# Two graph layers on one core: the first attention step in paired logits, statistics tile by tile, shifts on GpSimd

## The chip, the cores and the metric

The kernel runs on one core of a Trainium2 chip. The metric is the device time of one execution in microseconds (us). A core has a matrix engine (TensorE, PE in the profile), a vector engine (VectorE, DVE), an engine for activation functions (ScalarE, ACT), a general one (GpSimd, POOL) and SyncE (SP), which here issues transfers. Each engine takes its instructions in a program order of its own and waits on semaphores for the others. TensorE writes to PSUM[...]; the other tiles lie in SBUF.

## The reference

Eight batches of x (2048 nodes x 256 features) pass two layers that share one adjacency matrix (2048 x 2048).

```python
h = relu(layernorm(x))
# layer 0: 4 heads of 64, softmax over each chunk of 256 keys by itself
q, k, v = h @ Wq.T + bq, h @ Wk.T + bk, h @ Wv.T + bv
scores = clip(q @ k.T / sqrt(64), -10, 10);  scores = where(adj == 0, -10, scores)
ctx = sum over 8 chunks of softmax(scores of the chunk) @ v of the chunk
x = x + layernorm(ctx @ Wo.T + bo + h) * gamma + beta
h = relu(layernorm(x))
# layer 1
g = h @ W;  e = leaky_relu(g @ a1 + (g @ a2).T, 0.01);  e = where(adj == 0, -1e9, e)
x = x + relu(softmax(e) @ g)
```

## The kernel before

All arithmetic is float32. The order of the work on each engine is written out by hand: an engine executes its instructions in the order in which the program's calls emit them.

**A batch.** A batch has three stretches: attention (layer 0), the layer change, and layer 1. The 2048 rows are cut in four blocks of 512 (`nb` = 0 to 3; the program calls the four block objects `zero`, `low`, `mid`, `last`), and a block in four tiles of 128 rows (`TB`). While one batch is worked on, the projections q, k, v of the next one (`ahead`) are prepared in its layer change, and the row statistics for them in layer 1 of the batch before (`far`). In the first batch, `ahead`'s statistics are taken during attention.

**Attention.** There are 32 steps (block, chunk of keys) for a batch. A step has four heads, in `ORDER`; heads in places 0 and 2 of it use one half of TensorE's rows, 1 and 3 the other half, so that two heads can be multiplied at once. For each head and step, `logits` (L400) multiplies into one of two PSUM tiles of scores (`ps_s`), `clip` (L440, VectorE) clips and masks them into `e`, which gives the PSUM tile back, and `exponentials` (L449, ScalarE) follows. `add` (L455, GpSimd) adds two key tiles, `sums` (L428) and `values` (L416) multiply on TensorE, `invert` (L460, L461, ScalarE) makes the reciprocal, `scale` (L470, VectorE) applies it and frees the banks of `values` (`ps_n`), and `gather` (L475) adds the product to the context by a transfer issued from GpSimd.

The steps are software-pipelined in frames. Frame f has two halves, `begin(f)` (half number 2f) and `end(f)` (half 2f+1), and works on steps f, f-1, f-2 and f-3 at once. Frames 0 and 1 of a batch have no older step to work on. In the first batch they come before the loop; in the others they are put between the last pieces of layer 1 of the batch before (`begin(0)` and `end(0)` after its piece 12 of 0 to 15, `begin(1)` after 13, `end(1)` after 14).

**Pieces beside attention.** What else has to be done is listed by half in `todo`. A piece marked `first` is emitted at the start of its half, one marked `pe` before or between the logits, all others later: those of a `begin` half come after clips 1 and 2 of the frame, those of an `end` half before clip 3. The class `Between` carries a block from attention to layer 1, with its halves counted from 16 (nb + 1):

- `output` (L577, TensorE) and `take` (L586, VectorE) make the attention's output in two PSUM banks and copy each out.
- `stats` (L259, L260, VectorE, on one tile of 128 rows at a time), `power` (L264, L265, ScalarE: Ln, then Exp) and `shift` (L269, VectorE, four numbers a row) make scale and shift of a norm.
- `scaled` (L607, ScalarE), `gamma`, `beta`, `bias` and `add` (L613, L617, L593, L621, on `self.adder`, which is GpSimd within attention) finish layer 0.
- `stats1`, `power1`, `shift1` and `norm1` (L283, ScalarE) are the norm for layer 1, `turn1` (L292, transposes) and `keep1` (L644, ScalarE) turn its result, `values` (L651) multiplies by W, and `keep` (L659 on ScalarE, L660 on VectorE) copies the bank out: the 256 features, and then the two products with a1 and a2.

**The layer change.** After the last frame the program emits what remains of the four blocks, mixed with `ahead`'s projections (`turn` L292 with the copies L330 and L332, `qk` L344 with the copies L348, `values` L358 with the copy L363). Four PSUM banks take turns there (`ps_m`: `ps_n` and `ps_t` alternately, two buffers each). A new user of a bank waits for the copy that frees it.

**Layer 1.** There are 16 pieces, four for each block. A piece is `weights` (L759 and L765, VectorE) and `products` (L782, TensorE). `finish` (L792 to L799) divides and adds to x. Of the accumulators, those of blocks 0 and 2 lie in the two `ps_s` tiles, those of blocks 1 and 3 in `ps_n` and `ps_t`.

Of the kernel before, what the change touches and what calls it, by code (L numbers as in the profile page):

```python
# [12 lines left out]
AF = mybir.ActivationFunctionType  # L13
ALU = mybir.AluOpType
# [14 lines left out]
def gnn_two_layers(  # L29
# [127 lines left out]
    def first(piece):  # L157

        piece.kind = "first"
        return piece  # L160
# [101 lines left out]
    def norm_power(mv, rn):  # L262

        nc.scalar.activation(rn[:, 0, :], mv[:, :, 1], AF.Ln, bias=eps)  # L264
        nc.scalar.activation(rn[:, 0, :], rn[:, 0, :], AF.Exp, scale=-0.5)  # L265

    def norm_shift(mv, rn):

        nc.vector.scalar_tensor_tensor(  # L269
            rn[:, 1, :], mv[:, :, 0], -1.0, rn[:, 0, :], op0=ALU.mult, op1=ALU.mult  # L270
        )

# [23 lines left out]
    class Projection:  # L296
        def __init__(self, b):
            self.b = b
            self.q = self.k = self.v = None
            self.x, self.mv, self.rn, self.hns, self.hT, self.pt = ({} for _ in range(6))  # L300

# [11 lines left out]
        def shift(self, nb):  # L313
            norm_shift(self.mv[nb], self.rn[nb])

# [63 lines left out]
    class Attention:  # L379
# [97 lines left out]
        def has(self, n):  # L477
            return 0 <= n < len(self.STEPS)

# [76 lines left out]
    class Between:  # L558
# [42 lines left out]
        def shift(self):  # L601
            norm_shift(self.mv, self.rn)

# [27 lines left out]
        def shift1(self):  # L631
            norm_shift(self.mv1, self.rn1)

# [40 lines left out]
        def beside(self, values):  # L674
# [7 lines left out]
                8: [pe(lambda: self.output(0)), pe(lambda: self.output(1)), lambda: self.beta(0)],  # L682
                9: [first(lambda: self.take(0)), first(lambda: self.take(1)), lambda: self.stats([0, 1])],
                10: [lambda: self.stats([2]), lambda: self.beta(1)],
                11: [lambda: self.stats([3])],
                12: [self.power],
# [11 lines left out]
            if self.nb == NNB - 2:  # L698
                return todo
            for t in range(TB):  # L700
                at(21 + t, lambda t=t: self.stats1([t]))
            at(25, self.power1)
            at(26, self.shift1)
            if self.nb == 1 or values:
                at(27, lambda: self.norm1(0))
                at(28, lambda: self.norm1(1))
            if values:
                for c in range(FC):
                    at(32, pe(lambda c=c: self.turn1(c)))
                    at(33, first(lambda c=c: self.keep1(c)))  # L710
                for t in range(TB):
                    at(36 + t // 2 * 2, pe(lambda t=t: self.values(t)))
                    at(37 + t // 2 * 2, first(lambda t=t: self.keep(t)))
# [183 lines left out]

    projs = {0: proj, 1: Projection(1)}
    att = Attention(proj)
    att.begin(0)  # L900
    att.end(0)
    att.begin(1)
    att.end(1)
    unfinished = None
    for b in range(B):
# [79 lines left out]

        last.adder = nc.vector
        mid.stats1(range(TB))
        low.ends(1)
        mid.power1()
        mid.shift1()  # L990
        if ahead:
# [20 lines left out]
            for t2 in range(2):  # L1012
                last.gamma(t2)
                last.add(t2)
            last.stats1(range(TB))
            mid.ends(1)
            last.power1()
# [7 lines left out]
            zero.norm1(1)  # L1025
            zero.ends(0)
            ahead.norm(3, 0)
            ahead.qk(2, 0)
            zero.ends(1)
            ahead.norm(3, 1)  # L1030
# [56 lines left out]
        for i, (nb, j4) in enumerate(pieces1):  # L1087
# [24 lines left out]
            if ahead and i == len(pieces1) - 4:  # L1112
                att = Attention(ahead)
                att.begin(0)
                att.end(0)
            if ahead and i == len(pieces1) - 3:
                att.begin(1)
            if ahead and i == len(pieces1) - 2:
                att.end(1)
        if ahead:  # L1120
# [33 lines left out]
```

## Time and profile before

| | us |
|---|---|
| median of 3 runs | 3686.9 (3685.46 to 3690.95) |
| the profiled execution | 3688.98 |
| its span in the trace | 3687.1 |

| engine | busy us | share |
|---|---|---|
| TensorE, matmuls | 3633.1 | 99% |
| TensorE, weight loads | 2202.9 | 60% |
| VectorE | 2600.7 | 71% |
| ScalarE | 1946.7 | 53% |
| GpSimd | 1781.4 | 48% |

The profile comes from one execution. In the timeline a line gives the start, the duration, the engine and the line of the kernel, the operation, what is written from what is read, how many instructions were merged (x), and in brackets the idle time before it with the engine and line that ended it. In the table of stretches the columns are the length, then the busy time of PE, PEld, DVE, ACT and POOL with the number of instructions, the granted clock of TensorE, the share of the DMA engines and GB/s. Ends of matmuls are modelled: successive matmuls overlap, so the distance of their starts tells more than their durations. A float32 matmul shows as two records.

### The profile page before, as it was taken

What the parts mean: (1) busy time and instruction counts of PE and PEld (TensorE: products, weight loads), DVE (VectorE), ACT (ScalarE), POOL (GpSimd) and SP (SyncE); (2) the same over time, 40 slices, a digit from 0 to 9 for tenths busy, and PEclk for the clock granted to TensorE, in tenths of its full rate; (3) what the DMA queues carried; (4) which work ended last, traced back from release to release, by engine and by line L of the source; (5) the groups of instructions that cost most, each with busy time, mean ns of one, the idle gap of its engine ahead of it and who ended that gap; (6) DMA issues with size and microseconds to landing.
All of it is one profiled execution on the core that took longest, in us unless ns stands there. A gap on an engine that the chain in (4) does not pass through costs nothing.

```text
span 3687.1 us, 99355 instructions
## 1 busy us (share of the span) xinstructions
PE 3633.1 (99%) x43952; PEld 2202.9 (60%) x43952; DVE 2600.7 (71%) x3959; ACT 1946.7 (53%) x2879; POOL 1781.4 (48%) x1098
## 2 busy tenths in 40 slices
PE   8999999999999999999999999999999999999999
PEld 4444785447754477545775457645586545865468
DVE  4887577865777666786667866678576785767766
ACT  4777416773167732676226762367613667147650
POOL 0678016870177702786027850378403774048731
PEclk9999999999999999999999999999999999999999
DMA  4554113340133401343113431134312332123321
GB/s 139 137 128 110 41 52 82 82 107 27 59 85 81 101 29 63 82 99 82 46 47 82 99 76 46 53 82 94 75 52 58 87 83 64 46 53 88 71 58 35
DMA packets 116641, 274.83 MB, mean 75 GB/s; under 512 B 9968, under 2 KB 75248, under 8 KB 108016
## 3 DMA queue, kind: packets, MB, share of 16 engines
q0 software_dynamic: 32256, 117.45, 17.4%
q1 hardware_dynamic: 83952, 151.01, 12.1%
q8 instruction: 344, 5.64, 0.6%
q14 instruction: 89, 0.73, 0.1%
HBM read 130.03 MB, written 20.97 MB: 41 GB/s over the span
## 4 chain that ended last, share of the span: by engine, by line
PE 90%; DVE 5%; ACT 2%; issue 1%; DMA 1%; POOL 1%; SPq 0%; POOLq 0%; DVEq 0%; ACTq 0%
PE ps_s L400 23%; PE ps_n L416 22%; PE ps_s L782 11%; PE ps_n L782 6%; PE ps_t L428 6%; PE ps_t L782 6%; PE ps_t L577 3%; PE ps_s L344 2%; PE ps_n L344 2%; PE ps_t L344 2%; DVE e L440 2%; PE ps_t L358 1%; PE ps_n L358 1%; PE ps_t L292 1%; PE ps_t L651 1%
## 5 line engine op out<-in xcount | busy, mean ns | idle before, releaser
L455 POOL TENSOR_TENSOR both<-e 128x1024 f32<-128x1024 f32 x512 | 1217.4, 2403 | 740.0 <-PE ps_s L400 248.4
L440 DVE SCALAR_TENSOR_TENSOR e<-ps_s,bound 128x1024 f32<-128x1024 f32 x1024 | 1218.7, 1219 | 399.7 <-PE ps_s L400 397.3
L400 PE MATMUL ps_s<-q,k 64*32 64x512 f32 x16384 | 1398.5, 591 | 4.2 <-DVE e L440 3.0
L449 ACT ACTIVATE e<-e 128x1024 f32<-128x1024 f32 x1024 | 1053.4, 1050 | 575.6 <-DVE e L440 553.3
L416 PE MATMUL ps_n<-e,v 64*32 64x512 f32 x16384 | 1182.5, 590 | 2.2 <-DVE prod L470 2.2
L416 PEld LDWEIGHTS ps_n<-e,v 64*32 64x32 f32 x16384 | 449.0, 107 | 501.6 <-issue 417.9
L400 PEld LDWEIGHTS ps_s<-q,k 64*32 64x32 f32 x16384 | 432.8, 106 | 478.2 <-issue 324.7
L799 POOL TENSOR_TENSOR x<-x,r 128x256 f32<-128x256 f32 x128 | 98.5, 770 | 1107.6 <-DVE rz L792 1039.3
L428 PE MATMUL ps_t<-both,ones 64*32 64x512 f32 x4096 | 533.7, 591 | 1.3 <-SPq L372 1.2
L782 PE MATMUL ps_s<-g,w 128*128 128x257 f32 x2048 | 448.7, 380 | 0.0
L782 PEld LDWEIGHTS ps_s<-g,w 128*128 128x128 f32 x2048 | 388.4, 190 | 55.0
L470 DVE TENSOR_TENSOR prod<-ps_n,rz 128x512 f32<-128x512 f32 x448 | 288.3, 685 | 164.5 <-PE ps_n L416 94.8
L765 DVE SCALAR_TENSOR_TENSOR w<-bound,w 128x1024 f32<-128x1024 int8 x256 | 313.7, 1225 | 8.7
L782 PE MATMUL ps_n<-g,w 128*128 128x257 f32 x1024 | 292.6, 382 | 0.0
L759 DVE TENSOR_SCALAR w<-src,cd 128x512 f32<-128x512 f32 x512 | 265.2, 560 | 36.2 <-ACT src L753 35.8
L782 PE MATMUL ps_t<-g,w 128*128 128x257 f32 x1024 | 290.1, 380 | 0.0
L460 ACT ACTIVATE rz<-ps_t 128x512 f32<-128x512 f32 x256 | 152.6, 596 | 179.6 <-PE ps_t L428 129.3
L475 POOL DMA_DIRECT2D ctxT<-prod x224 | 194.4, 868 | 54.8 <-DVE prod L470 53.3
L782 PEld LDWEIGHTS ps_n<-g,w 128*128 128x128 f32 x1024 | 192.7, 190 | 43.4 <-issue 17.6
L782 PEld LDWEIGHTS ps_t<-g,w 128*128 128x128 f32 x1024 | 194.0, 189 | 28.0
L428 PEld LDWEIGHTS ps_t<-both,ones 64*32 64x32 f32 x4096 | 117.9, 106 | 91.1 <-SPq L372 48.5
L461 ACT ACTIVATE rz<-rz 128x512 f32<-128x512 f32 x256 | 161.4, 631 | 8.1
(125 smaller groups left out, 2842.7 us busy)
## 6 DMA issues: line engine op xcount, KB each, us to landing
ctxT<-prod POOLq DMA_DIRECT2D x224, 512.0 KB, 4.8
bound<-bound_d SPq DMA_DIRECT2D x60, 1024.0 KB, 5.3
xp<-in_x_dram SPq DMA_DIRECT2D x60, 512.0 KB, 4.8
rows<-in_adj_dram SPq DMA_DIRECT2D x32, 512.0 KB, 4.7
x<-in_x_dram SPq DMA_DIRECT2D x32, 512.0 KB, 5.2
out_dram<-x SPq DMA_DIRECT2D x31, 512.0 KB, 2.9
bound_d<-bound SPq DMA_DIRECT2D x4, 1024.0 KB, 6.3
out_dram<-x SPq DMA_DIRECT2D x4, 128.0 KB, 1.7
```

Of the source, the lines that this page charges most:

```text
L344: nc.tensor.matmul(pp, w[:, di, do * P:(do + 1) * P], self.hT[nb][:, di, :], start=di == 0, stop=di == FC - 1,)
L400: nc.tensor.matmul(self.s[n, o][c * Q:(c + 1) * Q, kt, :], self.k[p][rows, at:at + Q], self.q[p][rows, nb * NB:(nb + 1) * NB], start=True, ...
L416: made.append(nc.tensor.matmul(self.num[n, c][h * Q:(h + 1) * Q, :], self.v[rows, j * KT + kt, at:at + Q], self.e[n, p][rows, i * KT + kt, :],
L428: nc.tensor.matmul(self.total[n][h * Q:(h + 1) * Q, :], ones[rows, :], self.both[n, h // 2][rows, h % 2, :], start=half == 1, stop=half == 0,)
L440: nc.vector.scalar_tensor_tensor(self.e[n, p][:, i * KT:(i + 1) * KT, :], self.s.pop((n, o)), -CLIP * SC, bounds[nb][:, j * KT:(j + 1) * K ...
L449: nc.scalar.activation(e, e, AF.Exp, scale=1.0 / SC)
L455: nc.gpsimd.tensor_tensor(self.both[n, p], e[:, 0], e[:, 1], op=ALU.add)
L470: nc.vector.tensor_tensor(dst[:, c, :], self.num.pop((n, c)), self.rz[n], op=ALU.mult)
L475: nc.gpsimd.dma_start(self.ctxT[nb], self.prod.pop(n), accum_op=ALU.add)
L759: nc.vector.tensor_scalar(w[:, i, :], self.src[nb], self.cd[:, 0, j:j + 1], self.cd[:, 1, j:j + 1], op0=ALU.mult, op1=ALU.max,)
L765: nc.vector.scalar_tensor_tensor(two, bounds1[nb][:, j - 1:j + 1, :], 0.0, two, op0=ALU.is_gt, op1=ALU.mult)
L782: nc.tensor.matmul(accs[t][:, 0:F + 1], w[:, i, t * P:(t + 1) * P], g[:, j, :], start=j == 0, stop=j == NT - 1,)
```

## The change

1. `Attention.early` replaces frames 0 and 1 of each batch. Its three parts emit the logits of step 0 two heads at a time (0 with 1, 2 with 3, alternating row halves), the clips and exponentials between, and the logits of head 0 of step 1. The places in layer 1 stay (after pieces 12, 13 and 14).
2. `norm_power` gets a third ScalarE instruction, which copies the scale with its sign turned. `norm_shift` becomes a multiplication of two operands, on an engine that is passed in: GpSimd for the blocks in attention and for the second batch's projections, VectorE otherwise.
3. In `beside`, statistics are spread out: `stats` of tiles 0 and 1 follow each one `take`, tile 2 comes in the same half, tile 3 one half later; `stats1` goes from four successive halves (21 to 24) to 20, 22, 26 and 28, and `power1`, `shift1`, `norm1`, `turn1` and `keep1` follow later.
4. In the layer change, the value products and bank copies of `low` and of `mid` stand tile by tile between the statistics of `mid` and of `last`, and `zero`'s transposes stand behind the q projection of `ahead`'s block 2 instead of before it.

```diff
         nc.scalar.activation(rn[:, 0, :], rn[:, 0, :], AF.Exp, scale=-0.5)
-
-    def norm_shift(mv, rn):
-
-        nc.vector.scalar_tensor_tensor(
-            rn[:, 1, :], mv[:, :, 0], -1.0, rn[:, 0, :], op0=ALU.mult, op1=ALU.mult
-        )
+        nc.scalar.activation(rn[:, 1, :], rn[:, 0, :], AF.Copy, scale=-1.0)
+
+    def norm_shift(engine, mv, rn):
+
+        engine.tensor_tensor(rn[:, 1, :], rn[:, 1, :], mv[:, :, 0], op=ALU.mult)
...
+        def early(self, part):
+
+            if part == 0:
+                for kt in range(KT):
+                    self.logits(0, 0, kt)
+                    self.logits(0, 1, kt)
+            elif part == 1:
+                for o in range(2):
+                    self.clip(0, o)
+                    self.exponentials(0, o)
+                for kt in range(KT):
+                    self.logits(0, 2, kt)
+                    self.logits(0, 3, kt)
+            else:
+                self.clip(0, 2)
+                self.exponentials(0, 2)
+                self.clip(0, 3)
+                for kt in range(KT):
+                    self.logits(1, 0, kt)
+                self.add(0, 0)
...
-                9: [first(lambda: self.take(0)), first(lambda: self.take(1)), lambda: self.stats([0, 1])],
-                10: [lambda: self.stats([2]), lambda: self.beta(1)],
-                11: [lambda: self.stats([3])],
+                9: [
+                    first(lambda: self.take(0)), first(lambda: self.stats([0])),
+                    first(lambda: self.take(1)), first(lambda: self.stats([1])), lambda: self.stats([2]),
+                ],
+                10: [lambda: self.stats([3]), lambda: self.beta(1)],
...
-            for t in range(TB):
-                at(21 + t, lambda t=t: self.stats1([t]))
-            at(25, self.power1)
-            at(26, self.shift1)
+            for t, n in enumerate((20, 22, 26, 28)):
+                at(n, lambda t=t: self.stats1([t]))
+            at(29, self.power1)
+            at(30, self.shift1)
             if self.nb == 1 or values:
-                at(27, lambda: self.norm1(0))
-                at(28, lambda: self.norm1(1))
+                at(31, lambda: self.norm1(0))
+                at(32, lambda: self.norm1(1))
             if values:
                 for c in range(FC):
-                    at(32, pe(lambda c=c: self.turn1(c)))
-                    at(33, first(lambda c=c: self.keep1(c)))
+                    at(34, pe(lambda c=c: self.turn1(c)))
+                    at(35, first(lambda c=c: self.keep1(c)))
...
+    projs[1].adder = nc.gpsimd
     att = Attention(proj)
-    att.begin(0)
-    att.end(0)
-    att.begin(1)
-    att.end(1)
+    for part in range(3):
+        att.early(part)
...
-        last.adder = nc.vector
-        mid.stats1(range(TB))
-        low.ends(1)
+        for block in blocks:
+            block.adder = nc.vector
+        for t in range(TB):
+            mid.stats1([t])
+            low.values(t)
+            low.keep(t)
...
-            last.stats1(range(TB))
-            mid.ends(1)
+            for t in range(TB):
+                last.stats1([t])
+                mid.values(t)
+                mid.keep(t)
...
-            zero.ends(0)
             ahead.norm(3, 0)
             ahead.qk(2, 0)
+            zero.ends(0)
             zero.ends(1)
...
             if ahead and i == len(pieces1) - 4:
                 att = Attention(ahead)
-                att.begin(0)
-                att.end(0)
-            if ahead and i == len(pieces1) - 3:
-                att.begin(1)
-            if ahead and i == len(pieces1) - 2:
-                att.end(1)
+            if ahead and i >= len(pieces1) - 4 and i < len(pieces1) - 1:
+                att.early(i - (len(pieces1) - 4))
```

More of the change, by code (lines that the diff above doesn't have):

```diff
@@ L299, in __init__ @@
             self.q = self.k = self.v = None
+            self.adder = nc.vector
             self.x, self.mv, self.rn, self.hns, self.hT, self.pt = ({} for _ in range(6))
@@ L313, in shift @@
         def shift(self, nb):
-            norm_shift(self.mv[nb], self.rn[nb])
+            norm_shift(self.adder, self.mv[nb], self.rn[nb])
         def norm(self, nb, t2):
@@ L601, in shift @@
         def shift(self):
-            norm_shift(self.mv, self.rn)
+            norm_shift(self.adder, self.mv, self.rn)
         def scaled(self, tiles):
@@ L631, in shift1 @@
         def shift1(self):
-            norm_shift(self.mv1, self.rn1)
+            norm_shift(self.adder, self.mv1, self.rn1)
         def norm1(self, t2):
```

## The prediction

> **What bounds the kernel now.** I read the page's totals first, then the busy time by stretch for one whole batch, then the timeline where TensorE has holes. Page, busy time and chain:
>
> ```profile
> span 3687.1 us, 99355 instructions
> PE 3633.1 (99%) x43952; PEld 2202.9 (60%) x43952; DVE 2600.7 (71%) x3959; ACT 1946.7 (53%) x2879; POOL 1781.4 (48%) x1098
> PE 90%; DVE 5%; ACT 2%; issue 1%; DMA 1%; POOL 1%; SPq 0%; POOLq 0%; DVEq 0%; ACTq 0%
> ```
>
> TensorE is the bound, but its 99% comes from modelled ends. I count starts instead: a 512-column matmul follows the last after 0.43 us, one of 256 columns after 0.216, a transpose after 0.109; of quarter matmuls (64*32, two row halves by four column groups) eight share 0.43. With the counts of the groups: 36864 quarters (L400, L416, L428) 1981 us; 5664 of 256 to 258 columns (L782, L577, L651, L358, L728) 1223; 512 of L344 220; 656 transposes and 256 of L211 86. That is 3510 of the 3687.1, so some 177 us are holes, or unpaired halves. One batch, stretch by stretch (layer change, layer 1, attention):
>
> ```profile
> 1278.80:1342.20 63.40, 60.60 (x256) 42.79 (x253) 26.67 (x71) 34.77 (x78) 3.38 (x3) 1.00 0.10 26
> 1342.20:1460.50 118.30, 118.30 (x602) 99.12 (x600) 89.90 (x174) 15.28 (x30) 15.34 (x16) 1.00 0.15 50
> 1460.50:1730.40 269.90, 269.77 (x4609) 131.38 (x4608) 203.28 (x241) 188.95 (x248) 203.63 (x118) 1.00 0.40 92
> ```
>
> By starts the layer change holds 58.8 us of work in 63.4, layer 1 115.5 in 118.2, attention 260.6 in about 268. What the change is worth is what it takes out of those 4.6, 2.7 and 8 us, batch by batch, and a short startup. Clock 1.00 throughout: no gain there.
>
> **Part 1: paired logits in the first step.** Timeline at the end of layer 1: the first step's logits L400 between the products L782.
>
> ```profile
> 1433.51 1.92 PE L400 MATMUL ps_s<-q,k 64*32 64x512 f32 x16
> ...
> 1442.50 1.95 PE L400 MATMUL ps_s<-q,k 64*32 64x512 f32 x32
> ...
> 1451.51 1.97 PE L400 MATMUL ps_s<-q,k 64*32 64x512 f32 x32
> ```
>
> Five units of 16 run as 16, 32, 32. The middle 32 alternate row halves in program order; the last 32 do not (head 3 whole, then the next step's head 0 whole), yet take the same 1.97 us: their starts lie two by two 0.06 us apart. The Trainium skill (TensorE: Matmul & The Clock Gate, "The mechanism") says matmuls keep strict program order; by it the last 32 would need seven slots of 0.43, 3.0 us, and pairing them would save 1.3 us in each of 7 batches, 9 us. The row decides: already paired. After the change the groups are 32, 32, 16: equal, so 0 us. The clips and exponentials move one piece earlier, but TensorE is full around 1460, so nothing follows. The second PSUM tile of scores that step 0 now needs at 1433.5 is free by 1430.2 (ScalarE's last L795).
> Startup, batch 0, is different: there L400 at 73.73 waits in order behind a clip, so the second clip starts at 74.93 instead of 73.7. The new order clips at once; the fourth clip ends about 1 us earlier, and the mask conversions queued behind it (L203, to which TensorE's transposes wait) follow. Bounds 0 to 1.3; I take **-1.0 us**.
>
> **Part 2: bank copies between statistics, layer change.** Timeline:
>
> ```profile
> 1281.39 1.56 POOL L621 TENSOR_TENSOR x<-x,o 128x512 f32<-128x512 f32 x1
> 1281.79 1.03 PE L651 MATMUL ps_n<-w1s,hT 128*128 128x258 f32 x4
> 1282.98 0.43 DVE L259 BATCH_NORM_STATS2 stats<-x 128x6 f32<-128x256 f32 x1 [1.42 <-POOL x L621]
> 1284.25 0.66 PE L292 MATMUL ps_t<-ident,hn 128*128 128x128 f32 x4 [1.43 <-DVE sd L660]
> ...
> 1303.94 0.13 DVE L660 COPY sd<-ps_t 128x2 f32<-128x2 f32 x1
> 1304.12 0.66 PE L292 MATMUL ps_t<-ident,hn 128*128 128x128 f32 x4 [0.64 <-DVE sd L660]
> ...
> 1305.74 4.03 ACT L283 ACTIVATE hn<-x,rn 128x256 f32<-128x256 f32 x8
> 1309.83 0.33 PE L292 MATMUL ps_t<-ident,hn 128*128 128x128 f32 x1 [0.16 <-ACT hn L283]
> ```
>
> Hole A: TensorE is done at 1282.67 (1281.79 + 4 x 0.22) and waits to 1284.25 for a bank, whose 0.15 us copy stands behind four tiles of statistics, the third of which waits for GpSimd. Interleaved, copies 0 and 1 come at 1281.2 and 1282.0 and both transposes run at once; the next product needs copy 2, still behind that third tile: 1282.98 + 0.43 + 0.18 + 0.15, so 1283.9 instead of 1285.18: **1.29 us**.
> Hole B: done at 1303.33, next start 1304.12. The same cure; VectorE and ScalarE come 1.09 us earlier (1.29 less 0.2 for the new Copy, by L265's 205 ns). The value product of 1305.05 starts at 1302.9: 0.86 more, 2.15 together.
> Hole C: zero's transposes wait for eight L283 (1305.74 to 1309.77) and lose 1.04 us. ScalarE can't follow by the whole 2.15: its third-tile wait stays and it has the Copy. L283 would end at 1308.6, TensorE be there at 1306.4. The change puts a 3.44 us q projection in front, until 1309.8; but now transposes and value products of zero stand back to back, and between them ScalarE has still a norm (1.08), two q copies and two bank copies (0.57 each): the second operand at 1312.0, against TensorE at 1310.7. I get 1.12 lost instead of 1.04. Sum 2.15 - 0.08 = 2.07 a batch, **-14.5 us** over 7 batches; bounds 1.3 to 2.9 each (9 to 20). The eighth has no next batch to fill in: its transposes wait for ScalarE's norms anyway (2.84 us in the trace), and the copies and the Copy in three norm chains lengthen that: **+0.5**.
>
> **Part 3: statistics and shift in attention.** A frame of VectorE is 4 x 1.22 + 2 x 0.69 = 6.3 us against 8.05 of TensorE. Where extras bunch, the clip is late:
>
> ```profile
> 1236.05 1.55 POOL L617 TENSOR_TENSOR x<-x,beta_r 128x512 f32<-128x512 f32 x1
> ...
> 1236.37 1.25 DVE L269 SCALAR_TENSOR_TENSOR rn<-mv,rn 128x4 f32<-128x4 f32 x1
> 1237.55 0.42 DVE L259 BATCH_NORM_STATS2 stats<-o 128x6 f32<-128x256 f32 x1
> ...
> 1238.62 2.32 DVE L440 SCALAR_TENSOR_TENSOR e<-ps_s,bound 128x1024 f32<-128x1024 f32 x2
> ```
>
> The shift of four numbers took 1.25 us beside GpSimd's L617, 0.15 elsewhere. Then two tiles of statistics (0.53 each): the clip is about 0.6 late and the scores at 1241.0 lose 0.46 us. In the frame before, three tiles make it 0.2. Both occur for blocks 1 and 2: 1.32 a batch. After: statistics 0 and 1 lie in the two waits for the output products (1.15 and 1.03 us; the second tile ends at 1225.85, the clip's scores at 1226.38), the shift is gone, one tile follows. 7 x 1.32 = 9.2; batch 0, where VectorE is full with L203 at 250 to 266 and loses about 4 us, 2.5. Bounds 4 and 15; I take 11.7.
> Cost: norm1 of block 1 moves from halves 59/60 to 63/64, two times 1.08 us on ScalarE where scaled (2.07) and residual (2.1) already stand. The reciprocal L460 of 1256.25 moves to 1257.3, scale L470 from 1257.94 to 1258.6, and the values of 1259.35 need both banks: 0.6, and 0.2 for the sums; 0.8 x 8 = 6.4, bounds 0 and 13. Net **-5.3**. The moved power1 (Ln, Exp, now Copy: 0.29 + 0.21 + 0.2) lies before L460, which finds ScalarE idle for 0.9 to 1.1 us: 0; if that cover is gone, 0.2 each time. The later transposes of the last batch's block 0 (halves 34, 35) find their inputs a whole frame old: 0.
> The shift on GpSimd: no row has four elements there; L799 (256 elements) takes 721 ns, a 16-element memset 126, so 0.13 to 0.7, I take 0.15 to 0.3. It stands between gather and the add L455, before which GpSimd idles 2.63 us (1246.87): 0. The Trainium skill (GPSIMD Engine Reference, "Engine selection") speaks against it: two-input elementwise belongs on VectorE, about twice as slow on GpSimd. Twice 0.15 still fits the idle time; by the rule alone 40 shifts cost 6 us, by the row nothing. Moved DMAs: none.
>
> **Sum.** -1.0 - 14.5 + 0.5 - 5.3 = -20.3 against the profiled execution's 3688.98 us (span 3687.1): 3668.7. The median of the three runs is 2.1 lower: 3686.9 - 20.3 = **3666.6 us**. About 0.2% (7.4 us) is what a measurement can tell from no change.
>
> **Rivals.**
> 1. ScalarE is the next limit of the layer change: hole C takes back most of A and B (its eight norms not a bit earlier: 1.29 + 0.86 come back as waits). Then -1.0 - 5.3 and some 3 left: 3678. For: the chain goes through L283 for 3.9 us. Against: the q projection put in front covers 3.44. Chance 0.15.
> 2. Attention gains all and norm1 costs nothing (other waits lie later): 11.7 + 14.5 + 1 - 0.5 = 26.7, with upper bounds 34: 3653 to 3660. Chance 0.2.
> 3. Slower: GpSimd's shift waits for ScalarE's new Copy behind exponentials (2.19 us), and behind it stands the add L455, for which the sums L428 on TensorE wait. 5 shifts in 8 batches: each us over the 2.63 idle costs 40. From 0.5 us overrun it eats the 20 gained; at 1 us 3706. Against: Ln and Exp of 1242.93 end at 1243.44, the gather at 1244.2. Chance 0.04.
> 4. The statistics were no limit and all remains within noise: 0.04.
> My own case: 0.57, 3660 to 3674. Range with rivals 1 and 2: **3653 to 3678**. Faster by over 0.2% (below 3679.5): 0.91; within: 0.05; slower: 0.04.
>
> **What would show it.** Right: L292 at hole A waits under 0.2 us for L660; layer change 61.3 us instead of 63.4; L400 groups 32, 32, 16 at the same 1.9 us each; L269 gone, its successor on GpSimd before an idle add; "ps_s L400 <- DVE e L440" under 110.8 us; a new L651 wait for L644 of about 1 us at zero. Wrong: a layer change still over 63 (rival 1), L455 waiting for ScalarE's rn (rival 3), values L416 waiting over 1 us in frame 32 (norm1 dearer than 0.8).

## The result, and the profile after

The changed kernel took **3663.34 us** (median of 6 runs, 3661.12 to 3667.74), the kernel before 3687.22 beside it (6 runs, 3684.49 to 3691.91): ratio 0.9935, 95% interval 0.9922 to 0.9948, 23.9 us less. Forecast were 3666.6 us, a gain of 20.3, and a range of 3653 to 3678. Page of the changed kernel: span, busy time, chain.

```profile
span 3661.2 us, 99422 instructions
PE 3624.1 (99%) x43952; PEld 2209.7 (60%) x43952; DVE 2582.2 (71%) x3915; ACT 1959.1 (54%) x2975; POOL 1788.7 (49%) x1142
PE 95%; DVE 2%; ACT 1%; DMA 1%; issue 0%; POOL 0%; POOLq 0%; SPq 0%; DVEq 0%; ACTq 0%
```

The number of matmuls is the same. VectorE has 44 instructions fewer and GpSimd 44 more (the shifts), ScalarE 96 more (the copies). TensorE's part of the chain rises from 90 to 95%, and most of what the chain lost lay on VectorE (5% to 2%). The same batch in the three stretches (layer change, layer 1, attention; they are cut 0.5 us later than those of the kernel before, which leaves their lengths as they are):

```profile
1268.03:1329.04 61.01, 60.15 (x255) 42.99 (x254) 26.79 (x72) 35.04 (x81) 3.39 (x3) 1.00 0.10 26
1329.04:1447.22 118.18, 118.18 (x607) 98.59 (x613) 89.58 (x176) 16.48 (x34) 16.02 (x17) 1.00 0.15 50
1447.22:1716.40 269.18, 269.13 (x4604) 131.91 (x4592) 201.11 (x234) 188.53 (x252) 203.88 (x122) 1.00 0.41 92
```

The layer change went from 63.4 to 61.0 us. Layer 1 stood still. For attention one batch says little, since its waits move from batch to batch; sums over the eight batches are compared below. The line numbers have moved: L283 and L292 are now L282 and L291, the shift is L270, L577 to L660 are 21 higher (L621 is L642, L651 L672, L660 L681), and L749 to L799 are 23 higher.

**The layer change.** TensorE's own list of waits (us in total, times, longest), first in the kernel before, then in the changed kernel:

```profile
PE ps_t L292 <- DVE sd L660: 14.5, 14, 1.4
PE ps_t L292 <- ACT hn L283: 11.9, 29, 2.8
PE ps_t L651 <- ACT hT L644: 2.7, 8, 0.3
```

```profile
PE ps_t L291 <- ACT hn L282: 9.5, 12, 3.2
PE ps_t L672 <- ACT hT L665: 6.1, 15, 0.5
```

The transposes' wait for VectorE's bank copy ("DVE sd L660"), two waits in each of seven batches, is gone. Their wait for ScalarE's norms fell from 11.9 to 9.5 us. The wait of the value products for the operand turned last (L665, before L644) rose from 2.7 to 6.1 us. In the timeline of the changed kernel:

```profile
1270.42 1.03 PE L672 MATMUL ps_n<-w1s,hT 128*128 128x258 f32 x4
1271.29 0.60 PE L291 MATMUL ps_t<-ident,hn 128*128 128x128 f32 x4
1271.62 0.43 DVE L259 BATCH_NORM_STATS2 stats<-x 128x6 f32<-128x256 f32 x1 [1.30 <-POOL x L642]
...
1272.37 1.59 PEld L358 LDWEIGHTS ps_t<-wvT,hT 128*128 128x128 f32 x8 [0.28 <-DVE sd L681]
...
1292.94 4.03 ACT L282 ACTIVATE hn<-x,rn 128x256 f32<-128x256 f32 x8
...
1299.89 0.48 PE L672 MATMUL ps_t<-w1s,hT 128*128 128x258 f32 x1 [0.48 <-ACT hT L665]
```

The transposes start 0.87 us after the last four value products, which is those products' own time. VectorE still waits 1.30 us for GpSimd's third tile, but the copies for the first two tiles are done by then. The last line is the new wait at `zero`.

**The first step of logits** (timeline):

```profile
1419.79 1.95 PE L400 MATMUL ps_s<-q,k 64*32 64x512 f32 x32
1428.80 1.95 PE L400 MATMUL ps_s<-q,k 64*32 64x512 f32 x32
1437.81 1.92 PE L400 MATMUL ps_s<-q,k 64*32 64x512 f32 x16
```

32, 32 and 16, where it was 16, 32 and 32; each group lasts as before.

**The same frame of attention, and the shift** (timeline; first the pair of clips that begins this frame in the kernel before, then the changed kernel: the frame of GpSimd's `beta`, and a shift one frame later):

```profile
1234.10 2.36 DVE L440 SCALAR_TENSOR_TENSOR e<-ps_s,bound 128x1024 f32<-128x1024 f32 x2 [0.33 <-PE ps_s L400]
```

```profile
1223.44 2.36 DVE L440 SCALAR_TENSOR_TENSOR e<-ps_s,bound 128x1024 f32<-128x1024 f32 x2 [0.37 <-PE ps_s L400]
...
1226.27 0.40 DVE L259 BATCH_NORM_STATS2 stats<-o 128x6 f32<-128x256 f32 x1
...
1226.88 2.36 DVE L440 SCALAR_TENSOR_TENSOR e<-ps_s,bound 128x1024 f32<-128x1024 f32 x2
...
1233.12 0.50 POOL L270 TENSOR_TENSOR rn<-rn,mv 128x4 f32<-128x4 f32 x1
...
1235.56 4.73 POOL L455 TENSOR_TENSOR both<-e 128x1024 f32<-128x1024 f32 x2 [1.94 <-PE ps_s L400]
```

From one pair of clips to the next it is 3.44 us, with two tiles of statistics between; in the kernel before it was 4.52 (1234.10 to 1238.62), with the shift and two tiles. The shift takes 0.50 us on GpSimd and ends ahead of an idle 1.94 us. The shifts of `rn` on VectorE in the kernel before, and those on GpSimd in the changed kernel (`--source`: number, then shortest, median and longest duration in ns):

```profile
L269 DVE SCALAR_TENSOR_TENSOR rn<-mv,rn x64: 128/163/1290, 196.4 to 3573.9; 128x4 f32<-128x4 f32 x64
L270 POOL TENSOR_TENSOR rn<-rn,mv x40: 192/478/517, 194.5 to 3494.0; 128x4 f32<-128x4 f32 x40
```

The long ones have one thing in common. Of the 96 shifts of the kernel before (64 of `rn`, 32 of `krn`), 18 ran while GpSimd was in an addition or multiplication of a `Between` block (L617 sixteen times, L593 and L613 once each). All 18 ended 0.02 to 0.03 us after that instruction and took 0.77 to 1.30 us; the other 78 took 0.13 to 0.17 us. So the shift was not slow: it stood until GpSimd's instruction was through. In the rows of the prediction L617 ends at 1237.60 and the shift at 1237.62.

### The profile page after: what moved, and what is told of

Same layout as the page of the kernel before. It is cut to its first block, busy times and chain, and to the rows that moved or that the text cites. A ratio compares the mean times of both kernels' runs of the same rounds, so it can differ in the third digit from the quotient of the medians.

```text
span 3661.2 us, 99422 instructions
## 1 busy us (share of the span) xinstructions
PE 3624.1 (99%) x43952; PEld 2209.7 (60%) x43952; DVE 2582.2 (71%) x3915; ACT 1959.1 (54%) x2975; POOL 1788.7 (49%) x1142
## 4 chain that ended last, share of the span: by engine, by line
PE 95%; DVE 2%; ACT 1%; DMA 1%; issue 0%; POOL 0%; POOLq 0%; SPq 0%; DVEq 0%; ACTq 0%
PE ps_s L400 24%; PE ps_n L416 23%; PE ps_s L805 12%; PE ps_t L428 6%; PE ps_n L805 6%; PE ps_t L805 6%; PE ps_t L598 3%; PE ps_s L344 2%; PE ps_n L344 2%; PE ps_t L344 2%; PE ps_t L672 2%; PE ps_t L358 1%; PE ps_n L672 1%; PE ps_n L358 1%; PE ps_t L291 1%; DMA ctxT<-prod 1%
## 5 line engine op out<-in xcount | busy, mean ns | idle before, releaser
L440 DVE SCALAR_TENSOR_TENSOR e<-ps_s,bound 128x1024 f32<-128x1024 f32 x1024 | 1219.4, 1220 | 384.8 <-PE ps_s L400 383.8
L400 PE MATMUL ps_s<-q,k 64*32 64x512 f32 x16384 | 1364.9, 590 | 2.8 <-DVE e L440 2.6
L449 ACT ACTIVATE e<-e 128x1024 f32<-128x1024 f32 x1024 | 1050.6, 1049 | 560.8 <-DVE e L440 540.5
L416 PE MATMUL ps_n<-e,v 64*32 64x512 f32 x16384 | 1164.0, 590 | 2.4 <-DVE prod L470 2.4
L416 PEld LDWEIGHTS ps_n<-e,v 64*32 64x32 f32 x16384 | 447.0, 107 | 501.7 <-issue 395.5
L400 PEld LDWEIGHTS ps_s<-q,k 64*32 64x32 f32 x16384 | 433.5, 106 | 460.3 <-issue 325.8
L428 PE MATMUL ps_t<-both,ones 64*32 64x512 f32 x4096 | 537.5, 591 | 1.0 <-SPq L372 0.5
L470 DVE TENSOR_TENSOR prod<-ps_n,rz 128x512 f32<-128x512 f32 x448 | 288.7, 686 | 189.3 <-PE ps_n L416 85.1
L428 PEld LDWEIGHTS ps_t<-both,ones 64*32 64x32 f32 x4096 | 121.1, 106 | 93.7 <-SPq L372 53.0
```

Of the source, the lines that this page charges most:

```text
L400: nc.tensor.matmul(self.s[n, o][c * Q:(c + 1) * Q, kt, :], self.k[p][rows, at:at + Q], self.q[p][rows, nb * NB:(nb + 1) * NB], start=True, ...
L416: made.append(nc.tensor.matmul(self.num[n, c][h * Q:(h + 1) * Q, :], self.v[rows, j * KT + kt, at:at + Q], self.e[n, p][rows, i * KT + kt, :],
L428: nc.tensor.matmul(self.total[n][h * Q:(h + 1) * Q, :], ones[rows, :], self.both[n, h // 2][rows, h % 2, :], start=half == 1, stop=half == 0,)
L440: nc.vector.scalar_tensor_tensor(self.e[n, p][:, i * KT:(i + 1) * KT, :], self.s.pop((n, o)), -CLIP * SC, bounds[nb][:, j * KT:(j + 1) * K ...
L449: nc.scalar.activation(e, e, AF.Exp, scale=1.0 / SC)
L470: nc.vector.tensor_tensor(dst[:, c, :], self.num.pop((n, c)), self.rz[n], op=ALU.mult)
```

## The experiments

The table collects what the runs gave. The kernel before was measured anew beside each group of runs, and the ratio is to that time: 3687.22 us for the changed kernel, 3684.75 for e1 to e4, 3684.51 for e5 to e8, 3685.28 for e9 to e11, 3684.73 for e12. Gains of different groups are compared by it, not by the medians alone. Attention is the sum over eight batches, the layer change one batch of the first seven, both by starts of matmuls in the one profiled execution of each kernel.

| kernel | median us | ratio to before (95%) | attention | layer change |
|---|---|---|---|---|
| before | 3687.22 | 1 | 2172.3 | 63.37 |
| changed | 3663.34 | 0.9935 (0.9922 to 0.9948) | 2163.3 | 61.00 |
| e1 layer change alone | 3670.41 | 0.9959 (0.9945 to 0.9974) | 2167.6 | 61.01 |
| e2 pairing alone | 3683.67 | 0.9999 (0.9990 to 1.0007) | 2166.7 | 63.38 |
| e3 places of statistics alone | 3674.23 | 0.9971 (0.9960 to 0.9982) | 2161.3 | 63.38 |
| e4 shift on GpSimd alone | 3678.07 | 0.9982 (0.9975 to 0.9990) | 2159.5 | 63.61 |
| e5 changed, residual earlier | 3658.39 | 0.9926 (0.9911 to 0.9941) | 2158.5 | 61.01 |
| e6 changed, first step by heads | 3659.71 | 0.9932 (0.9917 to 0.9947) | 2160.8 | 61.00 |
| e7 changed, every frame by heads | 3660.26 | 0.9930 (0.9916 to 0.9945) | 2158.9 | 61.00 |
| e8 changed, zero's transposes back | 3667.54 | 0.9950 (0.9933 to 0.9967) | 2160.0 | 61.92 |
| e9 changed, gather before the add | 3868.89 | 1.0499 (1.0485 to 1.0513) | 2369.8 | 61.01 |
| e10 e1 and e4 together | 3657.45 | 0.9926 (0.9914 to 0.9938) | 2156.8 | 61.01 |
| e11 e5 and e7 together | 3659.72 | 0.9928 (0.9914 to 0.9941) | 2159.0 | 61.00 |
| e12 changed, early places only | 3655.92 | 0.9922 (0.9909 to 0.9936) | 2157.3 | 61.01 |

The layer change repeats to 0.02 us from batch to batch. Attention does not: before, e1 and e2 have the same code in the frames of steady work and give 2172.3, 2167.6 and 2166.7 (mean 2168.8); changed, e6 and e8 give 2163.3, 2160.8 and 2160.0 (mean 2161.4). So a difference of 5.6 us or less between two attention sums of single executions shows nothing by itself.

**e1, the layer change alone.** To the kernel before:

```diff
-        mid.stats1(range(TB))
-        low.ends(1)
+        for t in range(TB):
+            mid.stats1([t])
+            low.values(t)
+            low.keep(t)
...
-            last.stats1(range(TB))
-            mid.ends(1)
+            for t in range(TB):
+                last.stats1([t])
+                mid.values(t)
+                mid.keep(t)
...
-            zero.ends(0)
             ahead.norm(3, 0)
             ahead.qk(2, 0)
+            zero.ends(0)
             zero.ends(1)
```

> The kernel before with the layer change's part alone: copies of low and mid between the statistics, zero's transposes behind the q projection. Theory (parts add up; the layer change gives 2.4 us a batch by the removed bank waits): the layer change takes 60.8 to 61.0 us instead of 63.4 (the new Copy of 0.2 us isn't there), the last batch's 18.7 becomes at most 18.9, attention stays at 268 to 271, total 16 to 18 us less, near 3670. Rival 1 (ScalarE is the next limit there and the gain seen came from elsewhere, from attention): layer change over 62.5, total less than 6 us less. Rival 2 (the gain needs the moved statistics too): between the two.

Measured 3670.41 against 3684.75, 14.3 less, layer change 61.01. This part brings over half of the whole gain, and brings it alone: its stage has the same length in e1 and in the changed kernel. e1 doesn't have ScalarE's new copy, so that copy costs this stage nothing once the order is changed.

**e2, the pairing alone.** To the kernel before, at the end of layer 1 and in the same way at the start:

```diff
-                att.begin(0)
-                att.end(0)
-            if ahead and i == len(pieces1) - 3:
-                att.begin(1)
-            if ahead and i == len(pieces1) - 2:
-                att.end(1)
+            if ahead and i >= len(pieces1) - 4 and i < len(pieces1) - 1:
+                att.early(i - (len(pieces1) - 4))
```

> The kernel before with the first step in paired logits alone. Theory (row halves overlap already whatever the program order): three groups of 32, 32 and 16 of the same 1.9 us, nothing gained in layer 1; startup about 0.8 us earlier; total 0 to 2 us less, within noise of 3687. Rival (strict program order, pairing saves 1.3 us a batch and 20 us would come from it): layer 1 116.9 instead of 118.2, total 9 to 10 us less.

Measured: ratio 0.9999, within 0.1% of no change. Layer 1 took 118.18 us a batch against 118.21.

**e3, the places of the statistics alone.** To the kernel before (with tiles 2 and 3, and what follows `power1`, as in the change):

```diff
-                9: [first(lambda: self.take(0)), first(lambda: self.take(1)), lambda: self.stats([0, 1])],
+                9: [
+                    first(lambda: self.take(0)), first(lambda: self.stats([0])),
+                    first(lambda: self.take(1)), first(lambda: self.stats([1])), lambda: self.stats([2]),
...
-            for t in range(TB):
-                at(21 + t, lambda t=t: self.stats1([t]))
-            at(25, self.power1)
-            at(26, self.shift1)
+            for t, n in enumerate((20, 22, 26, 28)):
+                at(n, lambda t=t: self.stats1([t]))
+            at(29, self.power1)
+            at(30, self.shift1)
```

> The kernel before with the statistics' new places alone (shift stays on VectorE). Theory: the clips of the frames behind the outputs are no longer late by two tiles, but the shift of up to 1.3 us beside GpSimd's work stays; attention 0.4 to 1.0 us shorter a batch, less what the later norms on ScalarE cost in frames 31 and 32 (0.3); total 2 to 7 us less. Rival (the shift was the whole delay, the places matter nothing): 0 to 1 us less, or slower by the 2.5 us of the later norms.

Measured 10.5 us less, more than expected. Attention is at 2161.3, as short as in the changed kernel, though the shift still stood on VectorE. The frame of `beta` in e3 (timeline):

```profile
1228.86 2.36 DVE L440 SCALAR_TENSOR_TENSOR e<-ps_s,bound 128x1024 f32<-128x1024 f32 x2 [0.37 <-PE ps_s L400]
1230.80 1.56 POOL L617 TENSOR_TENSOR x<-x,beta_r 128x512 f32<-128x512 f32 x1
1231.13 0.42 DVE L259 BATCH_NORM_STATS2 stats<-x 128x6 f32<-128x256 f32 x1
...
1232.29 2.35 DVE L440 SCALAR_TENSOR_TENSOR e<-ps_s,bound 128x1024 f32<-128x1024 f32 x2
```

`shift1` of a block stood in the half of `beta(1)` of the next block (half 26 of the one is half 10 of the other). The new places move it to half 30, away from L617: 10 of the 96 shifts of e3 last over 0.2 us (beside L613 or L593) instead of 18, and from one pair of clips to the next it is 3.43 us here too.

**e4, the shift on GpSimd alone.** To the kernel before (`adder` as in the change):

```diff
+        nc.scalar.activation(rn[:, 1, :], rn[:, 0, :], AF.Copy, scale=-1.0)
...
-        nc.vector.scalar_tensor_tensor(
-            rn[:, 1, :], mv[:, :, 0], -1.0, rn[:, 0, :], op0=ALU.mult, op1=ALU.mult
-        )
+        engine.tensor_tensor(rn[:, 1, :], rn[:, 1, :], mv[:, :, 0], op=ALU.mult)
```

> The kernel before with the shift on GpSimd and the Copy on ScalarE alone. Theory: the 1.25 us instructions are gone from VectorE at two places a batch (and at four in the first batch), clips come up to 1.1 us earlier there and TensorE gains about 0.4 us at each; total 4 to 8 us less; layer change longer by 0.2 to 0.4 a batch for the Copy in three norm chains, which takes 1.5 to 3 of that back. Rival (GpSimd's queue is held up by the shift, adds and sums come late): L455 waiting for ScalarE's rn, total equal or longer.

Measured 6.7 us less, attention 2159.5. The frame of `beta` in e4 (timeline):

```profile
1228.19 2.36 DVE L440 SCALAR_TENSOR_TENSOR e<-ps_s,bound 128x1024 f32<-128x1024 f32 x2 [0.33 <-PE ps_s L400]
1230.46 0.42 DVE L259 BATCH_NORM_STATS2 stats<-o 128x6 f32<-128x256 f32 x1
...
1231.62 1.23 DVE L440 SCALAR_TENSOR_TENSOR e<-ps_s,bound 128x1024 f32<-128x1024 f32 x1
```

Again 3.43 us from pair to pair, with two tiles of statistics at their old places. So e3 and e4 cure the same late clip, either of them alone as well as both together (4.52 us before, 3.44 changed), and their gains cannot be added. The extra ScalarE copy shows where it is on the path: with the old order the layer change is 0.24 us longer a batch (63.61), 1.7 us over seven.

**e5, is the late norm1 what costs in frame 32?** To the changed kernel:

```diff
-        at(STEPS2 - 1, lambda: last.residual(0))
-        at(STEPS2, lambda: last.residual(1))
+        at(STEPS2 - 4, lambda: last.residual(0))
+        at(STEPS2 - 3, lambda: last.residual(1))
```

> The changed kernel with the residual's norms (L282 for last, two times 1.08 us) at halves 60 and 61 instead of 63 and 64. Theory (crowding of ScalarE in frames 31 and 32 costs 0.35 us a batch after the change): attention 0.3 to 0.4 us shorter a batch, total 2 to 4 us less than the changed kernel's 3663.3, near 3660.5; the wait of L470 for the reciprocal L461 in frame 32 (0.80 us) is gone. Rival (it's the bank switches to the q projection that lose there, not ScalarE): no difference, 3663. Rival 2 (the block's x has not landed at half 60, ScalarE waits for it): longer.

Measured 3658.39. What TensorE loses in a stretch of one frame (8.05 us), counted by starts as a mean of batches 1 to 6, is 0.09 and 0.92 us at +242 and +250 us after the batch's first value product against 0.23 and 1.10 in the changed kernel, so 0.32 a batch. Such a count moves by some 0.2 us with where the stretches are cut. In the changed kernel's timeline of that frame:

```profile
1243.51 1.08 ACT L282 ACTIVATE hn<-x,rn 128x256 f32<-128x256 f32 x2
1244.50 1.08 ACT L282 ACTIVATE hn<-x,krn 128x256 f32<-128x256 f32 x2
1246.75 1.29 DVE L470 TENSOR_TENSOR prod<-ps_n,rz 128x512 f32<-128x512 f32 x2 [0.80 <-ACT rz L461]
```

Two norms back to back on ScalarE, then the reciprocal, and the scale waits for it. The crowding is there, at a price of about 0.3 a batch. By the medians e5 gains 26.1 us on the kernel before, the changed kernel 23.9; the intervals overlap.

**e6, first step head by head.** To the changed kernel, in `early`:

```diff
-                for kt in range(KT):
-                    self.logits(0, 0, kt)
-                    self.logits(0, 1, kt)
+                for o in range(2):
+                    for kt in range(KT):
+                        self.logits(0, o, kt)
```

> The changed kernel with the first step's logits in program order head after head (both key tiles of one head, then of the other) instead of alternating. Theory (row halves overlap without alternation in the program): the groups of 32 last 1.9 to 2.0 us as before, total 3663 within noise. Rival (strict program order): each group of 32 needs 7 slots, 3.0 us instead of 1.7, at two places in 8 batches: 20 us more, 3684.

Measured 3659.71. Timeline of the two groups of 32, with all 16 of one head before the 16 of the next:

```profile
1417.90 2.05 PE L400 MATMUL ps_s<-q,k 64*32 64x512 f32 x32
1427.02 1.97 PE L400 MATMUL ps_s<-q,k 64*32 64x512 f32 x32
```

2.05 and 1.97 us against 1.95 paired by hand. Layer 1 is 0.13 us a batch longer. Each of these groups has two matmuls that report a head done. In the order emitted they would be the 16th and the 32nd; in the trace they start as the 28th and the 32nd. So the sentence that an engine executes its instructions in the order of the calls ("The kernel before") does not hold here for TensorE: the second head's matmuls start between those of the first.

**e7, the same in every frame.** To the changed kernel, in `begin`:

```diff
-                for kt in range(KT):
-                    self.logits(f - 1, 1, kt)
-                    self.logits(f - 1, 2, kt)
+                for o in range(1, 3):
+                    for kt in range(KT):
+                        self.logits(f - 1, o, kt)
```

> The changed kernel with the pair of logits of every frame (heads 1 and 2 of a step) head after head instead of alternating. Theory: row halves overlap by themselves; head 2 waits for a clip, and head 1 no longer stands half behind it, so the same or a little less, 3650 to 3664. Rival (strict program order): 1.3 us more in each of 248 frames, about 3985.

Measured 3660.26, attention 2158.9. The order written by hand is worth nothing that can be measured in 31 steps of each batch either. With strict order of the two row halves e7 would have taken about 3985 us, so this run speaks most strongly against it.

**e8, zero's transposes back in front of the projection.** To the changed kernel:

```diff
+            zero.ends(0)
             ahead.norm(3, 0)
             ahead.qk(2, 0)
-            zero.ends(0)
             zero.ends(1)
```

> The changed kernel with zero's transposes in their old place, in front of the q projection. Theory (after the removed bank waits ScalarE's eight norms are 2.0 us behind TensorE, and the projection in front covers that): zero's transposes wait 2.5 to 3 us for L282, the wait for L665 of 0.9 us goes, layer change 62.4 to 63.0 instead of 61.0, total 10 to 14 us more than 3663, near 3675. Rival (the norms would have been in time, the place is indifferent): 61.0, 3663.

Measured: layer change 61.92, 0.92 a batch more, less than expected. The gain on the kernel before is 17.0 us where the changed kernel has 23.9, and 7 times 0.92 is 6.4 of that difference. Timeline, e8:

```profile
1295.65 4.03 ACT L282 ACTIVATE hn<-x,rn 128x256 f32<-128x256 f32 x8
1298.26 0.33 PE L291 MATMUL ps_t<-ident,hn 128*128 128x128 f32 x1 [0.44 <-ACT hn L282]
```

The transposes come while ScalarE is in the middle of its eight norms and follow them one by one. Without this move ScalarE would take back 0.92 of the 2.37 us, and the other 1.45 would stay.

**e9, gather before the add.** To the changed kernel:

```diff
+            if self.has(f - 3):
+                self.gather(f - 3)
             if self.has(f - 2):
                 self.add(f - 2, 1)
-            if self.has(f - 3):
-                self.gather(f - 3)
```

> The changed kernel, but GpSimd issues the gather transfer before the frame's second add instead of behind it. Two accounts of the holes that are left in attention (8 batches of 270.4 us against 260.6 us of matmul starts, about 10 us a batch, of which some 2.5 are in the steady frames). Account 1, the transfer: VectorE's scale L470 waits for the transfer of the frame before (65 waits, 72.1 us), because that one is issued up to 1.8 us after its data are ready, behind an add of 2.4 us. Then the waits L470 <- DMA ctxT<-prod fall below 20 us, the attention sum falls by 2 to 8 us and the time is 3655 to 3661. Account 2, VectorE itself: the clips with their extras fill the frame and the wait for the transfer only takes up what would be lost anyway; then the waits for the transfer disappear too, but the time stays within 2 us of the changed kernel's 3663. Against both: the add comes up to 0.9 us later, and the sums L428 wait for it; if that is not covered, L428 loses up to 0.9 us in a frame and the time is over 3670.

Measured 3868.89, ratio 1.0499: the case that spoke against both accounts. Waits of e9 by all engines, then a timeline:

```profile
PEld ps_t L428 <- POOL both L455: 232.4, 174, 3.2
POOL ctxT L475 <- DVE prod L470: 123.4, 87, 6.6
```

```profile
1607.51 1.29 DVE L470 TENSOR_TENSOR prod<-ps_n,rz 128x512 f32<-128x512 f32 x2
1609.10 0.87 POOL L475 DMA_DIRECT2D ctxT<-prod  x1 [0.87 <-ACT e L449]
1609.71 2.66 POOL L455 TENSOR_TENSOR both<-e 128x1024 f32<-128x1024 f32 x1
```

GpSimd is idle from 1608.23. The gather's operand is there when the scale L470 ends (1608.80), the add's when the exponential L449 ends (1608.98, which the row names): the two become ready together, the gather goes first, and the add starts at 1609.71, 0.7 us late. In other frames the gather, and the add behind it, waits for the scale itself (the second line above). TensorE's sums L428 wait for the add; in the changed kernel that wait of the weight loads was 2.5 us in all. The attention sum is 208 us over the mean of the changed kernel's kind (2161.4), 0.93 us for each of 224 gathers. Whether the transfer's wait costs anything in the changed kernel stays open, because this edit swapped it for a larger one.

**e10, no new places.** The edits of e1 and e4 together.

> The kernel before with two parts of the change: the layer change's order and the shift on GpSimd with the third ScalarE instruction. The statistics stay at their old places, the first step head by head. The shift alone brought 6.6 us and the places alone 10.5, the layer change alone 14.3: a sum of 31, while the whole change brought 23.9. If the two attention parts cure the same late clips, this kernel loses nothing without the new places: 3660 to 3665, attention over 8 batches 2159 to 2164, layer change 61.0 to 61.2. If the parts add and something else eats 7 us in the whole change, it lies between, at 3666 to 3671, attention at 2166 or more.

Measured 3657.45, 27.8 us under the kernel before, attention 2156.8: nothing is lost without the places, for the changed kernel gained 23.9. By the mean of e4 and e10 (2158.1) the shift alone takes 10.7 us out of attention, and the places (7.5 alone, e3) add nothing to it.

**e11, e5 and e7 together.**

> The changed kernel with residual three halves earlier (60 and 61 instead of 63 and 64), so that the late norms of block 1 meet less ScalarE work, and with the middle two heads of every frame multiplied head by head. Each alone gave 3658.4 and 3660.3 against 3663.3. If both gains are real and add: 3655 to 3658. If they are scatter between executions of attention: 3658 to 3663.

Measured 3659.72, no better than either. The hole at +242 is closed again (-0.01 and 0.94 us at the two places), but a gain of 2.6 us (8 times 0.32) could not be seen within the scatter of attention.

**e12, the early places without the late ones.** To the changed kernel (and `norm1`, `turn1`, `keep1` at their old halves):

```diff
-            for t, n in enumerate((20, 22, 26, 28)):
-                at(n, lambda t=t: self.stats1([t]))
-            at(29, self.power1)
-            at(30, self.shift1)
+            for t in range(TB):
+                at(21 + t, lambda t=t: self.stats1([t]))
+            at(25, self.power1)
+            at(26, self.shift1)
```

> The changed kernel with the later places of stats1, power1, shift1, norm1, turn1 and keep1 taken back (halves 21 to 24, 25 to 28, 32 and 33), and the early places of stats kept (behind each take). The kernel without any new place took 3657.5 us against 3663.3 with all of them, and its attention is 3.2 us shorter in batches 1 to 6 at +161 to +169 and +242 to +250 us of the batch. If the late places are what costs and the early ones gain (at +153 and +217 us, 0.2 us each in batches 1 to 7 and 0.5 in batch 0), this kernel is the fastest: 3652 to 3657, with the holes at +161 under 0.2 us and at +242 near 0. If the early places cost (the clips behind them come later), +161 stays at 0.4 and the time is 3659 to 3664.

Measured **3655.92**, the lowest of all: ratio 0.9922 (0.9909 to 0.9936) against the changed kernel's 0.9935 (0.9922 to 0.9948). That is 28.8 us under its own kernel before, where the changed kernel has 23.9. The intervals overlap, so that it beats the kernel before is shown, and that it beats the changed one is likely only. Frame 32 of e12 (timeline):

```profile
1240.21 1.08 ACT L282 ACTIVATE hn<-x,krn 128x256 f32<-128x256 f32 x2
1242.93 1.29 DVE L470 TENSOR_TENSOR prod<-ps_n,rz 128x512 f32<-128x512 f32 x2 [0.27 <-PE ps_n L416]
```

One pair of norms in front of the reciprocal instead of two, and the scale waits for TensorE instead of ScalarE. The holes at +242 and +250 are 0.07 and 0.95. The one at +161 stayed at 0.48: that half of the expectation failed, so it does not come from the late places. In e10, which has no new place at all, the hole at +161 is only about 0.1 by such a count of starts, while those at +153 and +217 are each about 0.2 larger than in e12. So the early places move a loss from two frames to a third and gain nothing on the whole.

## Why the prediction was right, point by point

Both gains were there, and both came out larger than forecast: the layer change for the reasons given, attention with a mechanism that was right about the late clip and wrong about what it takes to cure it.

**Part 1.** Paired logits in layer 1 at 0: right (e2, e6, e7). The row of the kernel before was read rightly, against strict order; e2 moved layer 1 by 0.03 us a batch. Startup at -1.0: the first L416 came at 84.34 instead of 85.18 us, but over all the kernels here this time lies between 83.4 and 87.3, so a gain of this size can't be told from none.

**Part 2.** -14.5 predicted, -16.6 found (7 times 2.37). Hole A gave 1.35 for 1.29, hole B 0.85 for 0.86. The first is closer than the working deserves: its sum (1282.98 + 0.43 + 0.18 + 0.15) makes 1283.74 and not 1283.9, which is 1.44 us. The value projection L358 does start 1.44 us earlier, and the next product after it (L577, now L598) 1.35. The mis-sized term was hole C: 1.12 us lost was forecast where 1.04 had been, and about 0.9 was lost, so it gave 0.16 (2.37 less A and B) instead of costing 0.08. The working let the second operand of `zero` come 1.3 us after TensorE; it came 1.1 us after (at 1300.33, TensorE being ready at 1299.24). The last batch's +0.5 can't be seen: its change took 18.70 us before and 19.22 after, but 17.45 to 19.22 over all the kernels.

**Part 3.** Net -5.3 predicted. By the means of like kernels attention fell by 7.4 (2168.8 to 2161.4), in the two profiled executions by 9.0. Its two terms can be told apart in e12: without the late places attention is at 2157.3, so statistics and shift gained 11.5 where 11.7 was forecast, and the late places took back 4.1 where 6.4 was. The 2157.3 is one execution, and the scatter is up to 5.6 us: that the first term agrees to 0.2 is luck, and the 4.1 by itself would show nothing. The second term is the one mis-sized all the same: norm1 in frame 32 was priced at 0.8 us a batch, and the holes from +225 to +250 (batches 1 to 6) are about 0.4 larger in the changed kernel than in e12, or 0.3 by e5. That makes some 3 us in eight batches where 6.4 was forecast. What the prediction did not see is that statistics and shift are one remedy, not two: it counted the shift, held up by L617, and the tiles of statistics behind it as delays to be removed each, but the clip is in time as soon as the shift is away from L617 (e3, e4), and the places add nothing (e10).

**GpSimd's shift.** Duration forecast 0.15 to 0.3 us, measured 0.48 (median of 40). It shows no cost all the same, as forecast from the idle time before the add: where 6 us dearer was the alternative, e4 gained 6.7. The shift waited for ScalarE's copy in two places, 0.8 us in all.

**The sum by spans.** Startup -0.8, layer change -16.6, last batch +0.5, layer 1 -0.1, attention -9.0: -26.0, against 3661.2 - 3687.1 = -25.9. By the medians 23.9.

**The rivals.** 1 (ScalarE takes back what A and B give) is refuted as it stood, since the layer change is at 61.0; e8 shows its size without the reordering, 0.92 of 2.37. 2 (norm1 free) was half right: 0.3 to 0.4 instead of 0.8. 3 (GpSimd's queue held up by the shift) did not happen, but e9 shows what an instruction that becomes ready late costs in that place: 0.93 us for each gather, all of it on TensorE. The prediction had taken the idle 2.63 us before the add as slack. For an instruction that is ready early in it, such as the shift, it is; for one that becomes ready together with the add, it is not. 4 (noise) is refuted by the interval of the ratio.

**What would show it.** Transposes at hole A without a wait for L681: yes. Layer change 61.3: 61.0. Groups 32, 32, 16: yes. "ps_s L400 <- DVE e L440" under 110.8: 85.8. A wait of about 1 us at `zero`: 0.48 in TensorE's row, 0.72 in that of its weights. Values waiting over 1 us in frame 32: no, the scale ahead of them waits 0.80.

## What to carry to other kernels

Read a bank's holder from the wait list of the bound engine, then look at what stands in program order in front of the copy that frees it: here an engine three steps away (GpSimd's third tile) held two finished banks, and interleaving the copies with the statistics gave 1.35 us at the first place and 0.85 at the second. When a short instruction takes eight times as long in some places, list what the other engines ran just then: moving it to another place or another engine may both do. When two edits act on the same late instruction, test each alone before you add up their gains, and keep the one that delays nothing else. Idle time in front of an instruction hides only work whose operands are already there.

## What the runs showed of the hardware

- Matmuls of two row halves overlap whether they alternate in the program or come sixteen by sixteen: 32 in 1.95 us and in 1.97 to 2.05, and in the second case the last matmul of the first head starts as 28th of 32.
- VectorE's shift (four numbers a row, two operands in SBUF) took 0.13 to 0.17 us by itself. In 18 of 18 cases where it met a GpSimd addition or multiplication of 128x512 it ended 0.02 to 0.03 us after it, up to 1.30 us long. A tile of statistics beside the same L617 kept its 0.42 us (e3). On GpSimd the shift took 0.19 to 0.52 us, 0.48 in the median.
- Issuing an accumulating transfer of 512 KB held GpSimd for 0.86 us (0.82 to 1.18) in the changed kernel.
- Attention varied by up to 5.6 us between executions of like code, while the layer change repeats to 0.02 us.
